# Block order of GpSimd's residual and bias additions in a fused graph attention and graph convolution kernel

## The chip, the cores and the metric

The kernel runs on one core of a Trainium2 chip. The metric is the device time of one execution in microseconds (us), the median of several runs. A core has five engines that run their own instruction streams side by side and wait for each other through semaphores: TensorE (PE: matmuls; PEld: its weight loads), VectorE (DVE), ScalarE (ACT), GpSimd (POOL) and SyncE (SP), which here only issues transfers (DMAs). They share an on-chip memory of 128 partitions (SBUF); matmuls write to a second one, PSUM, which GpSimd doesn't read here.

## What is computed

Two layers over 32 batches (B) of 512 nodes with 512 features (N = D = 512), in float32. Layer 0 is masked attention with 8 heads of 64, layer 1 a graph convolution with the symmetrically normalised adjacency. Each has a residual and a layer norm without weights.

```python
def _layernorm(x, axis=-1, eps=1e-5):
    m = jnp.mean(x, axis=axis, keepdims=True)
    v = jnp.var(x, axis=axis, keepdims=True)
    return (x - m) / jnp.sqrt(v + eps)

# layer 0
q, k, v = ((x @ W + b).reshape(B, N, 8, 64) for W, b in ((Wq, bq), (Wk, bk), (Wv, bv)))
scores = jnp.einsum('bihd,bjhd->bhij', q, k) / 8
scores = scores + jnp.where(adj == 0, -1e9, 0.0)[None, None]
out = jnp.einsum('bhij,bjhd->bihd', softmax(scores), v).reshape(B, N, 512)
x = _layernorm(x + out)
# layer 1
deg_inv_sqrt = jnp.where(deg > 0, rsqrt(deg), 0.0)      # deg = adj.sum(axis=1)
norm_adj = adj * deg_inv_sqrt[:, None] * deg_inv_sqrt[None, :]
x = _layernorm(x + jnp.einsum('nm,bmo->bno', norm_adj, x @ weight) + bias)
```

## The kernel before

The 512 nodes of a batch are four blocks of 128 (NT = 4, one block per 128 partitions); the eight heads are four pairs (G = 4), taken in the order 0, 2, 1, 3. Projections and the last product with the convolution's weight use a scheme of seven block products instead of eight (`seven`, `second`), whose pieces are written out and combined by VectorE, ScalarE and GpSimd.

The main loop (line 819) runs over all pairs of heads of all batches, 128 steps. Step k issues the scores of its own pair and the values (`values`, line 408) of the pair before it. In each of two halves of a step, eight score matmuls write two PSUM tiles `sc`; VectorE takes each into a tile `e` with the cap and the mask (line 384), ScalarE takes the exponential in place (line 387), and GpSimd adds the `e` tiles up in `acc` (`accumulate`, line 389), from which the softmax's sums are folded. There are two `sc` buffers in PSUM, so the second half's score matmuls wait until VectorE has emptied the first half's. Projections and other products use three PSUM buffers named `mm`.

Between the two score halves other work is placed. While the scores of batch b are made, the steps also hold the projections for batch b + 1 and the rest of batch b - 1. They are lists of pieces, `main` (seven pieces for the values, then seven and five or more for keys and queries), with side pieces put behind the piece of a given number by the dictionary `beside` (line 849). `cut` (line 769) deals the list over the four steps of a batch, eight matmul pieces to a step. Instructions are kept in the order of the program on each engine (`InOrder`, line 34; all of them appear under line 44 in the profile). The order of the program is thus the order of every engine's queue.

The side pieces that matter here come from `finish(b)` (line 498), which ends layer 0 of one batch:

- `inverse_all` makes the reciprocals of the softmax's sums, `inv`.
- `scale` (line 537, VectorE): the attention's output `yT`, block i, times `inv`. The profile shows it as `yT<-yT,inv`.
- `add` (line 544, GpSimd): plus the residual, `yT<-yT,xr`.
- `measure` (line 564, VectorE): mean and variance of each block, `st<-yT` and `mv<-st`.
- `root` (line 569): `ve` and `nmu` on VectorE, then reciprocal root `rstd` and `add` on GpSimd, all four blocks in one.
- `norm` (line 574, ScalarE): the normalised block `yT<-yT,add,rstd`, and its scaled, rounded high part `hi<-yT,dis`.
- `low` (line 592, VectorE): the low part that `hi` leaves, `lo<-yT,dis,hi`. TensorE multiplies the adjacency by both parts (`mm<-adjT,hi` and `mm<-adjT,lo`).
- `lift` (line 597, GpSimd): plus the layer 1 bias, `yT<-yT,b_r`.
- `grow` (line 600, ScalarE): times the root of the degree, `yT<-yT,rdeg`; layer 1 adds its products to this.

Each of these runs once per block, in the order that `block` (line 604) gives: 0, 1, 2, 3. They are placed like this:

```python
6: rest[6:] + f["scale"][:2], 7: f["scale"][2:] + f["add"],
8: measure[:2] + put_off, 9: measure[2:], 10: f["root"] + put_off, 11: norm[:1],
12: norm[1:2] + low[:1], 13: norm[2:3] + low[1:2], 14: norm[3:] + low[2:3],
15: low[3:] + f["lift"], 16: put_off + grow[:2], 17: put_off + grow[2:], 18: turn0 + f["judge"],
```

`put_off` is a held back accumulation of `e` tiles on GpSimd (`more`, line 784). Piece 7 is the first projection piece of keys and queries; it stands last in its step's share, so the next step's scores follow behind `add`. Piece 15 is again the last of its share, and the scores follow behind `lift`. In the projection pieces for keys and queries the piece with number 10 is the one in which VectorE makes `u` (line 358), and TensorE's piece 13 takes over the PSUM buffer that this frees.

The batches 0 to 29 pass through this dictionary. Batch 30 is finished in lists of its own (lines 864 to 880), and batch 31 in the lines from 919 on; it scales and adds in pairs of heads (`add_pair`) instead of with `scale` and `add`. `general` (line 952) stands by for inputs out of range and doesn't run here.

Of the kernel before, what the change touches and what calls it, by code (L numbers as in the profile page):

```python
# [49 lines left out]
def unshifted(  # L50
# [29 lines left out]
    B, N, D = x.shape  # L80
    NT = N // P
# [395 lines left out]
    def statistics(y, mv):  # L477
        st = small.tile([P, 6], F32, name="st")
        vector.bn_stats(st, y)
        vector.bn_aggr(mv, st)  # L480
# [17 lines left out]
    def finish(b):  # L498


        t = {}
# [60 lines left out]
                )  # L562

        def measure(i):
            if i == 0:
                t["mv"] = small.tile([P, NT, 2], F32, name="mv")
            statistics(YT[b][:, i, :], t["mv"][:, i, :])

# [35 lines left out]
        def block(f):  # L604
            return [(0, f, (i,)) for i in range(NT)]

        return dict(
            early=[(0.6, inverse, ((0,),))], late=[(0.6, inverse, ((1,),)), (0.6, turn_values, (ORDER[-1],))],
            pairs=[[(0, add_pair, (i, g)) for i in range(NT)] for g in ORDER],
            halves=[(0, root, (0, 2)), (0, root, (2, 2))],  # L610
            inverse=[(0.6, inverse_all, ())], scale=block(scale), add=block(add), measure=block(measure), root=[(0, root, ())],
            judge=[(0, judge, ())], norm=block(norm), low=block(low), lift=block(lift), grow=block(grow),
        )

    def weave(side, main):
# [203 lines left out]
    for k in range(S + 1):  # L819
        b, at = divmod(k, G)  # L820
        if at == 1:
# [10 lines left out]
            if b == 0:  # L832
# [10 lines left out]
                shares = cut(side, (4, 4, 4, 4))  # L843
            elif b < B - 1:
                f, c = finish(b - 1), convolve(b - 1)
                norm, low, grow, measure = f["norm"], f["low"], f["grow"], f["measure"]

# [11 lines left out]
                if b < B - 2:  # L859
                    side += put_off + s[:1] + put_off + s[1:3] + turn1[1:2] + s[3:4] + turn1[2:3] + s[4:5]  # L860
                    side += turn1[3:4] + s[5:6] + c["measure"][:1] + turn1[4:] + s[6:] + c["measure"][1:2]
                    rest = c["measure"][2:] + c["root"] + c["store"]
                    shares = cut(side, (8, 8, 8, 8))
                else:
                    held, h, last = c, s, finish(b)
                    scale, add = last["scale"], last["add"]
                    side += h[:1] + last["inverse"] + h[1:2] + scale[:2] + h[2:3] + scale[2:] + add
                    shares = cut(side, (8, 8, 8, 4))
            else:
                f, c, last = last, convolve(b - 1), finish(b)  # L870
                s, first, low, lift, pairs = c["second"], c["first"], f["low"], f["lift"], last["pairs"]
                within = low[:1]
# [47 lines left out]
    norm, low, lift, block, pairs, extend = end["norm"], end["low"], end["lift"], e["block"], end["pairs"], c["extend"]  # L920
# [310 lines left out]
```

## Time and profile before

| | us |
|---|---|
| median of 3 runs (lowest to highest) | 2856.01 (2855.47 to 2856.58) |
| the profiled execution | 2858.47 |
| its span, first to last instruction | 2856.4 |
| TensorE busy in the span | 2817.5 |
| VectorE busy | 2301.6 |
| GpSimd busy | 1846.0 |
| ScalarE busy | 1046.8 |

The mean granted clock of TensorE in the profiled execution was 0.997. The groups of instructions that the change concerns, all on tiles of 128 partitions by 512 float32 elements; smallest, median and largest duration are from the view of one tile's instructions, the busy time from the list of groups:

| instruction | engine | count | ns, min / median / max | busy us |
|---|---|---|---|---|
| `yT<-yT,inv` (scale) | VectorE | 124 | 676 / 1243 / 1759 | 159.3 |
| `yT<-yT,xr` (add) | GpSimd | 124 | 1263 / 1652 / 1730 | 192.8 |
| `st<-yT` (measure) | VectorE | 124 | 659 / 664 / 690 | 83.2 |
| `lo<-yT,dis,hi` (low) | VectorE | 124 | 732 / 1235 / 1621 | 150.0 |
| `yT<-yT,b_r` (lift) | GpSimd | 124 | 1269 / 1278 / 1745 | 171.2 |

Rows of the timeline give start, duration, engine, operation, output and inputs, the number of like instructions merged in the row, and in brackets how long the engine sat idle before and what ended that. Consecutive instructions of one engine overlap by some tens of ns in the records, so a step is read from one start to the next.

### The profile page before, as it was taken

Reading aid. Unit: us, or ns where it says so; the run is one execution under the profiler, and the core shown is the slowest. Engines: PE = TensorE matmul, PEld = TensorE weight load, DVE = VectorE, ACT = ScalarE, POOL = GpSimd, SP = SyncE. Lnnn points to the kernel's source line nnn. Section 1 sums busy time; section 2 is a strip of 40 time slices with the busy share of each in tenths; the row PEclk is TensorE's granted clock in tenths of the full one; section 3 lists DMA queues with packets and bytes.
Section 4 is the critical chain, followed back from the end, with each engine's and each line's share of the span. In section 5 each row is a group of like instructions: output and inputs, shape, how many; then the busy total and the mean of one; then the engine's idle time right before and its main releaser. Section 6 shows DMA issues by size and latency. Waiting matters only on the chain.

```text
span 2856.4 us, 34678 instructions
## 1 busy us (share of the span) xinstructions
PE 2817.5 (99%) x12540; PEld 1865.2 (65%) x12540; DVE 2301.6 (81%) x3201; ACT 1046.8 (37%) x1323; POOL 1846.0 (65%) x1174
## 2 busy tenths in 40 slices
PE   8999999999999999999999999999999999999997
PEld 6566666666666666666666666666666666666655
DVE  5878877888778887788887788877888778788787
ACT  2333333343333433333333334333343333333344
POOL 3666666766666666666666676666666666666666
PEclk9999999999999999999999999999999999999999
DMA  4111122111221112221112211122112222111211
GB/s 118 32 29 48 49 56 46 41 47 49 59 56 42 37 48 56 56 45 41 49 48 58 51 41 41 50 58 56 41 37 51 53 56 45 41 49 48 59 38 50
DMA packets 379108, 141.05 MB, mean 49 GB/s; under 512 B 277808, under 2 KB 345392, under 8 KB 378928
## 3 DMA queue, kind: packets, MB, share of 16 engines
q1 hardware_dynamic: 377776, 137.17, 20.1%
q8 instruction: 101, 1.65, 0.2%
q10 hardware_dynamic: 1152, 1.57, 0.2%
q14 instruction: 79, 0.65, 0.1%
HBM read 71.83 MB, written 33.55 MB: 37 GB/s over the span
## 4 chain that ended last, share of the span: by engine, by line
PE 78%; DVE 19%; issue 2%; POOL 0%; DMA 0%; ACT 0%; DVEq 0%; POOLq 0%; ACTq 0%
PE mm L44 52%; PE sc L44 13%; PE av L44 12%; DVE yT L44 5%; DVE e L44 5%; DVE st L44 3%; DVE acc L44 1%; DVE u L44 1%; DVE mv L44 1%; DVE yb L44 1%; DVE v L44 1%; DVE kq L44 1%; DVE xT L44 0%; DVE plainT L44 0%; POOL xT L44 0%
## 5 line engine op out<-in xcount | busy, mean ns | idle before, releaser
L44 ACT ACTIVATE e<-e 128x1024 f32<-128x1024 f32 x512 | 540.8, 1057 | 1166.2 <-DVE e L44 1137.2
L44 POOL TENSOR_TENSOR acc<-acc,e 128x1024 f32<-128x1024 f32 x248 | 588.9, 2375 | 188.3 <-ACT e L44 181.0
L44 DVE SCALAR_TENSOR_TENSOR e<-sc,maskT 128x1024 f32<-128x1024 f32 x512 | 597.5, 1207 | 22.1 <-PE sc L44 21.9
L44 PE MATMUL sc<-kq 64*128 64x512 f32 x2048 | 523.2, 623 | 3.5 <-DVE e L44 3.3
L44 PE MATMUL mm<-xT,wk 128*128 128x256 f32 x1792 | 476.3, 388 | 13.7 <-DVE u L44 11.3
L44 PE MATMUL av<-e,v 128*64 128x512 f32 x2048 | 467.9, 598 | 0.0
L44 PE MATMUL mm<-xT,wq 128*128 128x256 f32 x1792 | 460.7, 380 | 0.0
L44 POOL TENSOR_TENSOR acc<-e 128x1024 f32<-128x1024 f32 x126 | 297.2, 2358 | 230.4 <-ACT e L44 230.4
L44 PEld LDWEIGHTS mm<-xT,wk 128*128 128x128 f32 x1792 | 327.8, 190 | 143.1 <-issue 73.1
L44 PE MATMUL mm<-wv,xT 128*128 128x256 f32 x1792 | 404.3, 383 | 1.7 <-DVE xT L44 1.1
L44 PEld LDWEIGHTS mm<-wv,xT 128*128 128x128 f32 x1792 | 335.6, 190 | 72.3 <-issue 25.4
L44 PEld LDWEIGHTS mm<-xT,wq 128*128 128x128 f32 x1792 | 341.1, 190 | 46.5
L44 PEld LDWEIGHTS sc<-kq 64*128 64x128 f32 x2048 | 171.3, 186 | 290.7 <-issue 150.9
L44 PEld LDWEIGHTS av<-e,v 128*64 128x64 f32 x2048 | 135.5, 136 | 316.2 <-issue 293.4
L44 PE MATMUL mm<-w,zT 128*128 128x256 f32 x992 | 224.9, 379 | 0.7 <-ACT side L44 0.7
L44 POOL TENSOR_TENSOR rstd<-ve,minus_half 128x4 f32<-128x4 f32 (+1 forms) x66 | 66.2, 1003 | 232.5 <-DVE nmu L44 232.5
L44 DVE TENSOR_TENSOR kq<-u,mm 128x512 f32<-128x512 f32 x128 | 87.8, 686 | 156.5 <-PE mm L44 153.0
L44 POOL TENSOR_TENSOR yT<-yT,b_r 128x512 f32<-128x512 f32 x124 | 171.2, 1392 | 63.3 <-DVE lo L44 63.3
L44 PEld LDWEIGHTS mm<-w,zT 128*128 128x128 f32 x992 | 188.2, 190 | 28.1 <-issue 1.5
L44 POOL TENSOR_TENSOR yT<-yT,xr 128x512 f32<-128x512 f32 x124 | 192.8, 1584 | 18.8 <-DVE yT L44 18.8
L44 PE MATMUL mm<-adjT,hi 128*128 128x512 f32 x496 | 202.0, 407 | 0.0
L44 PE MATMUL mm<-adjT,lo 128*128 128x512 f32 x496 | 196.0, 395 | 0.9 <-DVE lo L44 0.9
(141 smaller groups left out, 3382.8 us busy)
## 6 DMA issues: line engine op xcount, KB each, us to landing
out_dram<-y SPq DMA_DIRECT2D x127, 256.0 KB, 2.1
x<-in_x_dram SPq DMA_DIRECT2D x248, 128.0 KB, 2.9
yT<-yb SPq DMA_DIRECT2D x496, 64.0 KB, 2.5
xr<-in_x_dram SPq DMA_DIRECT2D x122, 256.0 KB, 3.3
wk<-in_L_gnn_Wk_dram SPq DMA_DIRECT2D x8, 128.0 KB, 5.0
wq<-in_L_gnn_Wq_dram SPq DMA_DIRECT2D x8, 128.0 KB, 4.3
yT<-in_adj_dram SPq DMA_DIRECT2D x1, 1024.0 KB, 6.4
w<-in_L_gnn_weight_dram SPq DMA_DIRECT2D x2, 512.0 KB, 8.1
```

The source lines that it names most:

```text
L44: return self.tc.keep_in_program_order(op(*args, **kwargs))
```

## The change

`finish` gets a second way to list a function's blocks, `behind`, which takes the last block first: 3, 0, 1, 2. `add` uses it always, `measure`, `lift` and `grow` for all batches but the last. `scale`, `norm` and `low` keep the order 0, 1, 2, 3. `measure` makes its tile at the first call, whichever block that is for.

The slices of lists that the dictionary takes (`measure[:2]`, `grow[:2]`) are unchanged; they now hold the blocks 3 and 0, the others 1 and 2. GpSimd's first `add` reads what the last `scale` wrote, and its first `lift` overwrites what the last `low` read; with the queues in order the other three of each stand behind it.

```diff
         def measure(i):
-            if i == 0:
+            if "mv" not in t:
                 t["mv"] = small.tile([P, NT, 2], F32, name="mv")
             statistics(YT[b][:, i, :], t["mv"][:, i, :])
...
         def block(f):
             return [(0, f, (i,)) for i in range(NT)]
 
+        def behind(f):
+
+
+            return [(0, f, (i,)) for i in (NT - 1, *range(NT - 1))]
+
         return dict(
...
-            inverse=[(0.6, inverse_all, ())], scale=block(scale), add=block(add), measure=block(measure), root=[(0, root, ())],
-            judge=[(0, judge, ())], norm=block(norm), low=block(low), lift=block(lift), grow=block(grow),
+            inverse=[(0.6, inverse_all, ())], scale=block(scale), add=behind(add),
+            measure=block(measure) if b == B - 1 else behind(measure), root=[(0, root, ())],
+            judge=[(0, judge, ())], norm=block(norm), low=block(low),
+            lift=block(lift) if b == B - 1 else behind(lift), grow=block(grow) if b == B - 1 else behind(grow),
         )
```

## The prediction

> **What bounds the kernel now.** I read the page first: engine shares, then the chain that ended last.
>
> ```profile
> PE 2817.5 (99%) x12540; PEld 1865.2 (65%) x12540; DVE 2301.6 (81%) x3201; ACT 1046.8 (37%) x1323; POOL 1846.0 (65%) x1174
> PE 78%; DVE 19%; issue 2%; POOL 0%; DMA 0%; ACT 0%; DVEq 0%; POOLq 0%; ACTq 0%
> ```
>
> TensorE (PE) is busy nearly always, yet a fifth of the chain lies on VectorE (DVE). So there are places where TensorE just keeps up with, or waits for, VectorE. The chain over 1556 to 1592 us shows where:
>
> ```profile
> 1557.88 5.11 DVE yT L44 x4
> 1562.99 2.27 DVE e L44 x2
> ...
> 1574.92 0.77 DVE u L44 x2
> 1575.73 5.45 PE mm L44 x24
> ```
>
> From the four scalings (yT) on, VectorE works without a break for 17.8 us, until TensorE waits for its `u`. The stage repeats every 87.80 us (the first scaling starts at 1470.00, then 1557.80), 30 times, for the batches 0 to 29; batch 30 has it in the tail.
>
> The timeline around the scalings, each asked for in a narrow window, VectorE and GpSimd (POOL):
>
> ```profile
> 1556.13 2.36 POOL L44 TENSOR_TENSOR acc<-acc,e 128x1024 f32<-128x1024 f32 x1
> 1557.80 1.24 DVE L44 TENSOR_TENSOR yT<-yT,inv 128x512 f32<-128x512 f32 x1
> ...
> 1558.96 0.68 DVE L44 TENSOR_TENSOR yT<-yT,inv 128x512 f32<-128x512 f32 x1
> 1559.12 1.65 POOL L44 TENSOR_TENSOR yT<-yT,xr 128x512 f32<-128x512 f32 x1 [0.63 <-DVE yT L44]
> ...
> 1559.57 1.75 DVE L44 TENSOR_TENSOR yT<-yT,inv 128x512 f32<-128x512 f32 x1
> 1560.73 1.72 POOL L44 TENSOR_TENSOR yT<-yT,xr 128x512 f32<-128x512 f32 x1
> ```
>
> A scaling with no GpSimd instruction starting before it takes 0.68 us. The third and fourth, beside residual additions, take 1.75; the first, beside the end of an accumulation, 1.24.
>
> What this costs TensorE I read from the starts of its rows:
>
> ```profile
> 1558.81 1.99 PE L44 MATMUL sc<-kq 64*128 64x512 f32 x8
> 1560.73 3.65 PE L44 MATMUL av<-e,v 128*64 128x512 f32 x16
> 1564.32 2.13 PE L44 MATMUL sc<-kq 64*128 64x512 f32 x8
> 1566.37 1.13 PE L44 MATMUL mm<-xT,wk 128*128 128x256 f32 x4
> ...
> 1573.38 1.11 PE L44 MATMUL mm<-xT,wk 128*128 128x256 f32 x4
> 1574.33 1.03 PE L44 MATMUL mm<-xT,wq 128*128 128x256 f32 x4
> 1575.73 1.13 PE L44 MATMUL mm<-xT,wk 128*128 128x256 f32 x4 [0.38 <-DVE u L44]
> ...
> 1577.57 1.03 PE L44 MATMUL mm<-xT,wk 128*128 128x256 f32 x4
> ...
> 1583.03 3.65 PE L44 MATMUL av<-e,v 128*64 128x512 f32 x16
> 1586.69 2.26 PE L44 MATMUL sc<-kq 64*128 64x512 f32 x8
> 1588.88 1.13 PE L44 MATMUL mm<-xT,wk 128*128 128x256 f32 x4
> ```
>
> Eight undisturbed score matmuls take 1.92 us to the next start (1558.81 to 1560.73), the values 3.59 (to 1564.32). A projection piece (four `wk` and four `wq` matmuls) takes 1.73: 1568.20 to 1569.93 in the same view. Against that TensorE loses:
> - 0.13: second scores, 1564.32 to 1566.37 is 2.05
> - 0.62: the piece at 1573.38, 2.35 to the next; it waits for the PSUM buffer that `u` frees
> - 0.11: the next piece, 1.84
> - 0.07: values at 1583.03, 3.66 to the next
> - 0.27: scores at 1586.69, 2.19 to the next
>
> Sum 1.20 us per batch. Times 30: 36.0 us of 2856.4. This is what a faster VectorE can give back.
>
> **What the Trainium skill says.** "SBUF — State Buffer", "Who interferes with whom": a VectorE instruction with two SBUF inputs contends with a GpSimd instruction that reads SBUF, and one with at most one SBUF input outside the two-port modes does not. The trace agrees: scaling (`yT` and `inv`) ranges from 676 to 1759 ns; `e` (PSUM and the mask) takes 1.21 us whether or not an addition runs. "Perfetto Trace Analysis", "Tensor Engine Instruction (MATMUL, LD_WEIGHTS)": the profiler's matmul end is an estimate. The trace agrees in that busy intervals overlap (1558.81 plus 1.99 is after 1560.73), so I use starts. "TensorE: Matmul & The Clock Gate", "Architectural detail: the array is 16× 32×32, not 1× 128×128": VectorE, ScalarE and GpSimd queues are strictly first in, first out. The in-order rows agree, and it is why block 3 in front holds all the other blocks.
>
> **The change, part by part.** No instruction is added or removed. The sequences on TensorE, VectorE, ScalarE and SyncE keep their kinds and shapes; only block numbers turn from 0,1,2,3 to 3,0,1,2. On GpSimd the first addition waits for the last scaling (or low part), and the next three have no wait for VectorE left. SyncE's DMAs are in the same order.
>
> *Additions.* The third and fourth scalings fall from 1.75 to 0.68: 2 x 1.07 = 2.14 us less on VectorE. The first keeps its 1.24, since the accumulation started before it. Scalings then end near 1560.86. GpSimd starts at 1560.94 and needs 4 x 1.24 (steps of the uncontended additions, 1.27 long and overlapping slightly), so to 1565.9; before, to 1565.4. The accumulation behind it started at 1566.49, held by ScalarE's exponential, which now comes 2.1 us sooner; so it starts at about 1565.9. The additions' new delay costs nothing: the first measurement, of block 3, is wanted at about 1568.9 and its addition ends at 1562.2. Without that slack of over 6 us each late microsecond would hold VectorE.
>
> *VectorE downstream.* The scores' `e` begin at 1560.8 instead of 1562.92, when their matmuls (1558.81 to 1560.73) are just done. Transpose, fold, `yb` follow; `yb` waits for the values, over at 1564.3, and is not late. The second `e` pair then runs 1566.0 to 1568.3 instead of to 1570.45, the measurements and `u` to 1573.5 instead of 1575.7. TensorE, without its losses, wants the buffer at 1574.98. Slack 1.4 us: the 0.13, 0.62 and 0.11 go.
>
> *Measure and root.* Same instructions, other block order; the reciprocal roots of all four blocks still start after the last. They come 2 us sooner.
>
> *Low parts and bias additions.* Two of the four low parts run beside a bias addition (mean over the batches 1361 and 1600 ns against 739 for the free one). Free: 0.62 + 0.86 = 1.48 us less. The first stays at 1.22 (an accumulation is beside it). Walking the chain: root 1573.7, first `hi` 1576.6, last `hi` 1581.9 (ScalarE's row of norms, `hi` and `e` copies is now what is late), last low 1582.7, then `e`: first score buffer free at 1583.8. TensorE wants it at 1585.77. Slack 2 us: the 0.07 and 0.27 go.
>
> *Bias additions' end.* Four after the last low part: 1582.8 to 1587.9, against 1586.9 before. Behind them stands the accumulation that waited for an exponential until 1588.93. It starts at 1587.9, sooner still; ScalarE's `grow` comes over 5 us later. Nothing shown waits.
>
> *Batch 30 in the tail.* The additions wait for a scaling beside `y<-yT,e`, about 0.4 us later; the last low part is 0.46 shorter, and TensorE waits 0.91 for it. GpSimd's later work slides by up to 2.3 us, into 1.77 us of idle time at 2801.6. I take 0, bounds -0.5 and +1.
>
> *Unknown.* TensorE's first `adjT` step is 0.42 us long in every batch, with 0.23 later. If that is a wait on VectorE rather than TensorE's own, another 0.19 x 30 = 5.7 us goes. I take 0; lower end 5.7. At the other side, each wait carries about 0.10 us of slower restart and small brushes beside it, which may be TensorE's own: bounded in the first rival.
>
> Sum: 1.20 x 30 = 36.0 less. Profiled span 2856.4 - 36.0 = 2820.4; its execution was 2858.47, 2.07 around the span, and the median of the runs 2856.01, 2.46 below it. Taken from the median: **2820**.
>
> **The rivals.** *Half goes.* Restarts (three of 0.10) and the brush of 0.08 before the long wait, with the rest small, stay since TensorE has them anyway. Then about 0.73 x 30 = 22 goes: 2834. For it: every restart after other changes of operand also shows 0.10. Against: undisturbed second scores lack it.
>
> *Nothing moves.* The freed 3.6 us of VectorE were hidden by TensorE at 99%: 2856. For it, the page's share; against, the start-to-start losses above, present in all 30 batches. That the change doesn't reach the order of issue is excluded by the GpSimd sequence.
>
> *Slower: the root comes late.* Block 3 in front makes GpSimd idle, then run four in a row; an accumulation that is thereby late would stand ahead of the root, and root, norm, `hi`, low, `e` would all wait. It decides when the second scores of the next step lose over 0.93 us more than now (what is gained elsewhere); each microsecond beyond costs 30. With the root 2 us later than now: (2 - 0.93) x 30 = 32, 2888. For it: that chain has no idle step once the root starts. Against: GpSimd idled 2.85 us before the root, for VectorE.
>
> **How the numbers follow.** Full gain 0.70 (2820; own range 2813 to 2827), half 0.18 (2834, 2826 to 2844), nothing 0.05, slower 0.07. The range for 8 in 10 is 2811 to 2838: full gain with the `adjT` step taken at nearly its end, and most of half. About 0.2%, 5.7 us, is what a measurement of this kernel can tell from no change. Faster by more 0.88, within 0.05, slower 0.07.
>
> **What would show it.** The period falls from 87.8 to 86.6; the third and fourth scaling read 0.68, low parts two and four 0.74; PE shows no wait on DVE `u`; second scores take 1.92 to the next start. Scalings short with the period at 87.8 would mean VectorE's lead ends in another wait, root or `hi`; scalings still at 1.75 would break the contention argument itself.

## The result and the profile after

| | before | changed |
|---|---|---|
| median of 4 runs, us | 2856.3 | 2821.38 |
| lowest to highest | 2855.47 to 2857.94 | 2821.04 to 2821.77 |
| profiled execution | 2858.47 | 2821.64 |
| its span | 2856.4 | 2819.7 |
| from one batch's first scaling to the next | 87.80 | 86.60 |

The ratio is 0.9877, 95% interval 0.9864 to 0.9889. The predicted time was 2820.

The two medians differ by 34.9 us; the prediction took off 36.0. From the page of the changed kernel, the engine shares and the chain that ended last:

```profile
PE 2792.0 (99%) x12540; PEld 1874.8 (66%) x12540; DVE 2177.5 (77%) x3201; ACT 1050.1 (37%) x1323; POOL 1786.4 (63%) x1174
PE 97%; DVE 2%; POOL 0%; issue 0%; DMA 0%; ACT 0%; POOLq 0%; DVEq 0%; ACTq 0%
```

TensorE's busy share is 99% as before, so it does not show the gain. The chain does: VectorE's share fell from 19% to 2%. Over 1530 to 1620 us, a little more than one batch, it lies on TensorE throughout; three of its 17 pieces:

```profile
1543.85 1.92 PE sc L44 x8
1545.77 14.01 PE mm L44 x64
1559.78 1.92 PE sc L44 x8
```

The timeline of the changed kernel for the stage that the prediction shows, VectorE and GpSimd (the first scaling starts at 1537.27, in the kernel before at 1557.80):

```profile
1537.27 3.03 DVE L44 TENSOR_TENSOR yT<-yT,inv 128x512 f32<-128x512 f32 x4
1540.22 2.34 DVE L44 SCALAR_TENSOR_TENSOR e<-sc,maskT 128x1024 f32<-128x1024 f32 x2
...
1552.21 0.84 DVE L44 SCALAR_TENSOR_TENSOR u<-e,step,mm 128x256 f32<-128x256 f32 x2
...
1561.24 0.75 DVE L44 SCALAR_TENSOR_TENSOR lo<-yT,dis,hi 128x512 fp32r<-128x512 f32 x1 [0.66 <-ACT hi L44]
1561.91 2.35 DVE L44 SCALAR_TENSOR_TENSOR e<-sc,maskT 128x1024 f32<-128x1024 f32 x2
...
1540.38 4.98 POOL L44 TENSOR_TENSOR yT<-yT,xr 128x512 f32<-128x512 f32 x4 [2.43 <-DVE yT L44]
...
1562.08 4.98 POOL L44 TENSOR_TENSOR yT<-yT,b_r 128x512 f32<-128x512 f32 x4 [5.25 <-DVE lo L44]
```

The same rows in the kernel before:

```profile
1557.80 5.19 DVE L44 TENSOR_TENSOR yT<-yT,inv 128x512 f32<-128x512 f32 x4
...
1574.84 0.84 DVE L44 SCALAR_TENSOR_TENSOR u<-e,step,mm 128x256 f32<-128x256 f32 x2
...
1585.42 2.34 DVE L44 SCALAR_TENSOR_TENSOR e<-sc,maskT 128x1024 f32<-128x1024 f32 x2
```

The four scalings take 3.03 us instead of 5.19, and GpSimd idles 2.43 us ahead of its additions. Counted from the first scaling, `u` comes at 14.94 us instead of 17.04, and the scores' `e` behind the low parts at 24.64 instead of 27.62. TensorE in the same stage:

```profile
1543.78 1.99 PE L44 MATMUL sc<-kq 64*128 64x512 f32 x8
1545.70 1.13 PE L44 MATMUL mm<-xT,wk 128*128 128x256 f32 x4
...
1552.71 1.03 PE L44 MATMUL mm<-xT,wk 128*128 128x256 f32 x4
...
1554.44 1.03 PE L44 MATMUL mm<-xT,wk 128*128 128x256 f32 x4
...
1556.17 1.03 PE L44 MATMUL mm<-xT,wk 128*128 128x256 f32 x4
...
1561.63 3.65 PE L44 MATMUL av<-e,v 128*64 128x512 f32 x16
1565.21 1.99 PE L44 MATMUL sc<-kq 64*128 64x512 f32 x8
1567.13 1.13 PE L44 MATMUL mm<-xT,wk 128*128 128x256 f32 x4
```

All five losses are gone: both scores take 1.92 us to the next start, the values 3.58, the pieces 1.73, and no bracket shows a wait for `u`. The same holds in the other batches. A batch has 388 steps from one matmul's start to the next; averaged over 29 batches, only eight of them differ by more than 12 ns between the two kernels. All eight lie at these five places, and together they are 1.20 us.

The view of the tile's instructions in the changed kernel (smallest, median, largest duration in ns, first and last start):

```profile
L44 DVE TENSOR_TENSOR yT<-yT,inv x124: 677/680/1764, 151.7 to 2724.2; 128x512 f32<-128x512 f32 x124
L44 POOL TENSOR_TENSOR yT<-yT,xr x124: 1261/1278/1292, 154.8 to 2729.7; 128x512 f32<-128x512 f32 x124
...
L44 DVE SCALAR_TENSOR_TENSOR lo<-yT,dis,hi x124: 734/752/1233, 170.5 to 2748.7; 128x512 fp32r<-128x512 f32 x124
L44 POOL TENSOR_TENSOR yT<-yT,b_r x124: 1262/1278/1294, 176.5 to 2753.2; 128x512 f32<-128x512 f32 x124
```

The 36.7 us of span are accounted for: 29 periods of 1.20 (34.8), 1.21 from the last of these to batch 30's first scaling, 1.36 in the start before the first scaling, and 0.64 given back in the tail. The first two are the change: 36.0. The start has the same instructions in the same order in both kernels (it took 153.03 us before and 151.67 after); in the kernels below it took anywhere from 150.96 to 153.38 us, so the 1.36 is within the scatter.

### The profile page after: what moved, and what is told of

The parts are those of the page before. It is cut to its first block, busy times and chain, and to the rows that moved or that the text cites. A ratio compares the mean times of both kernels' runs of the same rounds, so it can differ in the third digit from the quotient of the medians.

```text
span 2819.7 us, 34592 instructions
## 1 busy us (share of the span) xinstructions
PE 2792.0 (99%) x12540; PEld 1874.8 (66%) x12540; DVE 2177.5 (77%) x3201; ACT 1050.1 (37%) x1323; POOL 1786.4 (63%) x1174
## 3 DMA queue, kind: packets, MB, share of 16 engines
q8 instruction: 101, 1.65, 0.2%
## 4 chain that ended last, share of the span: by engine, by line
PE 97%; DVE 2%; POOL 0%; issue 0%; DMA 0%; ACT 0%; POOLq 0%; DVEq 0%; ACTq 0%
PE mm L44 64%; PE sc L44 17%; PE av L44 16%; DVE e L44 1%; DVE xT L44 0%; DVE plainT L44 0%; POOL xT L44 0%; POOL acc L44 0%; DVE st L44 0%; DVE y L44 0%; DMA xr<-in_x_dram 0%; DVE lo L44 0%; DVE kq L44 0%; DVE lost L44 0%; DVE ve L44 0%
## 5 line engine op out<-in xcount | busy, mean ns | idle before, releaser
L44 PE MATMUL sc<-kq 64*128 64x512 f32 x2048 | 510.1, 616 | 3.6 <-DVE e L44 3.5
L44 PE MATMUL mm<-xT,wk 128*128 128x256 f32 x1792 | 469.7, 384 | 2.4 <-issue 2.0
L44 POOL TENSOR_TENSOR yT<-yT,b_r 128x512 f32<-128x512 f32 x124 | 154.6, 1279 | 167.7 <-DVE lo L44 167.7
L44 POOL TENSOR_TENSOR yT<-yT,xr 128x512 f32<-128x512 f32 x124 | 154.4, 1278 | 73.6 <-DVE yT L44 73.6
```

What stands on the lines that cost most here:

```text
L44: return self.tc.keep_in_program_order(op(*args, **kwargs))
```

## The experiments

Each is compared in five rounds with runs of the kernel before on the same chip, which gave 2855.24 to 2856.15 us as medians. For the changed kernel the 2821.38 us from above are used. Close cases are read from the period, the mean time from one batch's first scaling to the next; the kernels given with 86.60 agree in it within 0.01 us.

### One half alone

**Additions and measurements only.**

```diff
-            lift=block(lift) if b == B - 1 else behind(lift), grow=block(grow) if b == B - 1 else behind(grow),
+            lift=block(lift), grow=block(grow),
```

> Additions and measurements with block 3 in front; bias additions and grow in the old order 0, 1, 2, 3, so two low parts run beside bias additions again (1.4 and 1.6 us). Theory (only waits at a PSUM buffer cost time, and VectorE has slack after the scalings): the scores behind the low parts come 0.9 us later than in the changed kernel, the first score buffer is still free 1.2 us before TensorE wants it, so the period stays 86.6 and the time is 2821 to 2823. Rival (each microsecond that VectorE saves is worth the same, 36 us for 2.14 + 1.48 us): 2821 + 15 = 2836.

Measured: 2821.36 us, ratio 0.9879 (0.9863 to 0.9894), period 86.60. VectorE's timeline of this kernel, where the first scaling starts at 1538.46:

```profile
1559.09 2.05 DVE L44 SCALAR_TENSOR_TENSOR lo<-yT,dis,hi 128x512 fp32r<-128x512 f32 x2
...
1562.44 1.61 DVE L44 SCALAR_TENSOR_TENSOR lo<-yT,dis,hi 128x512 fp32r<-128x512 f32 x1 [0.67 <-ACT hi L44]
1563.97 2.34 DVE L44 SCALAR_TENSOR_TENSOR e<-sc,maskT 128x1024 f32<-128x1024 f32 x2
```

The low parts are slow again (1.38 and 1.61 us), `e` comes at 25.51, 0.87 later than in the changed kernel, and the time is the same. So with the additions moved, moving the bias additions is worth nothing that can be measured. `e` still comes earlier than the 27.62 of the kernel before, and that is early enough.

**Bias additions and grow only.**

```diff
-            inverse=[(0.6, inverse_all, ())], scale=block(scale), add=behind(add),
-            measure=block(measure) if b == B - 1 else behind(measure), root=[(0, root, ())],
+            inverse=[(0.6, inverse_all, ())], scale=block(scale), add=block(add),
+            measure=block(measure), root=[(0, root, ())],
```

> Bias additions and grow with block 3 in front; additions and measurements in the old order, so the third and fourth scaling take 1.75 us again. Theory: the losses of 0.13, 0.62 and 0.11 us per batch at the second scores and at u stay, the 0.07 and 0.27 behind the low parts go: 0.34 x 30 = 10 us less than before, 2846. Period 87.46. Rival (each saved microsecond of VectorE is worth the same): 1.48 of 3.62, 15 us less, 2841.

Measured: 2846.6 us, ratio 0.9967 (0.9955 to 0.9979), period 87.47. TensorE's timeline of this kernel:

```profile
1567.96 1.11 PE L44 MATMUL mm<-xT,wk 128*128 128x256 f32 x4
1568.90 1.03 PE L44 MATMUL mm<-xT,wq 128*128 128x256 f32 x4
1570.31 1.13 PE L44 MATMUL mm<-xT,wk 128*128 128x256 f32 x4 [0.38 <-DVE u L44]
...
1581.19 1.99 PE L44 MATMUL sc<-kq 64*128 64x512 f32 x8
1583.11 1.13 PE L44 MATMUL mm<-xT,wk 128*128 128x256 f32 x4
```

The wait for `u` is as before; the scores behind the low parts take the undisturbed 1.92. The halves alone gain 35 and 10 us, both at once 35: the second gain is contained in the first, because moving the additions also brings the low parts forward by about 2 us.

### The wait or the block order

```diff
+        def touch():
+            last = small.tile([P, 32], F32, name="last", bufs=1)
+            gpsimd.tensor_copy(last, YT[b][:, NT - 1, :32])
+
+        def touch_low():
+            last = small.tile([P, 32], F32R, name="last2", bufs=1)
+            gpsimd.tensor_copy(last, LO[b][NT - 1][:, :32])
...
+            inverse=[(0.6, inverse_all, ())], scale=block(scale), add=[(0, touch, ())] + block(add),
+            measure=block(measure), root=[(0, root, ())],
...
+            lift=block(lift) if b == B - 1 else [(0, touch_low, ())] + block(lift), grow=block(grow),
```

> All blocks in the old order 0, 1, 2, 3; ahead of the additions GpSimd copies 32 columns of the last scaled block, and ahead of the bias additions 32 columns of the last low part, into a small tile nobody reads. So the wait is as in the changed kernel, the block order as before. Theory (what counts is that GpSimd waits for the last scaling and low part): 2821 to 2823, scalings 0.68, period 86.6. Rival (the order of the blocks itself, that is which measurement or grow comes first, is part of the gain): above 2826.

Measured: 2821.22 us, ratio 0.9877 (0.9862 to 0.9892), period 86.60. The timeline of this kernel:

```profile
1537.04 3.05 DVE L44 TENSOR_TENSOR yT<-yT,inv 128x512 f32<-128x512 f32 x4
...
1540.15 0.21 POOL L44 COPY last<-yT 128x32 f32<-128x32 f32 x1 [2.42 <-DVE yT L44]
...
1540.50 1.27 POOL L44 TENSOR_TENSOR yT<-yT,xr 128x512 f32<-128x512 f32 x1
```

A copy of 0.21 us that waits does all that the block order does. So the order in which the blocks are added and measured is no part of the gain; what counts is that GpSimd's queue stands until VectorE is through.

### How much VectorE may lose

**Half of the scalings' gain given back.**

```diff
-            inverse=[(0.6, inverse_all, ())], scale=block(scale), add=behind(add),
-            measure=block(measure) if b == B - 1 else behind(measure), root=[(0, root, ())],
+            inverse=[(0.6, inverse_all, ())], scale=block(scale), add=[(0, add, (i,)) for i in (1, 0, 2, 3)],
+            measure=block(measure) if b == B - 1 else [(0, measure, (i,)) for i in (1, 0, 2, 3)], root=[(0, root, ())],
```

> Additions and measurements in the order 1, 0, 2, 3, bias additions and grow with block 3 in front as in the changed kernel. GpSimd then starts after the second scaling; one scaling runs beside an addition and takes 1.75 instead of 0.68, so half of the 2.14 us comes back. Theory (slack of about 1.3 us at u, 2 us behind the low parts): all of it fits into the slack, 2821 to 2824, no wait of TensorE for u. Rival (the gain is in proportion to VectorE's saving): 1.07 of 3.62 us lost, 2821 + 11 = 2832.

Measured: 2822.27 us, ratio 0.9881 (0.9866 to 0.9896), period 86.60. The median scaling durations are 1227, 678, 677 and 1750 ns. One slow scaling per batch costs nothing in the period.

**Both given back in part.** The edit is the one just shown together with the first one, `lift=block(lift), grow=block(grow)`.

> Additions and measurements in the order 1, 0, 2, 3, bias additions and grow in the old order: one scaling at 1.75 and two low parts at 1.4 and 1.6 come back, 1.07 + 1.48 = 2.55 of the 3.62 us that the change saves on VectorE. Theory (slack of 1.4 us at u, of 2.06 us at the scores behind the low parts, where 1.07 + 0.87 = 1.94 us are used): still 2820 to 2824, period 86.6 to 86.7. Rival (in proportion): + 25, 2846.

Measured: 2824.03 us, ratio 0.9891 (0.9875 to 0.9908), period 86.70. The timeline of this kernel, VectorE and TensorE, first scaling at 1538.17:

```profile
1563.16 1.61 DVE L44 SCALAR_TENSOR_TENSOR lo<-yT,dis,hi 128x512 fp32r<-128x512 f32 x1 [0.71 <-ACT hi L44]
1564.69 2.34 DVE L44 SCALAR_TENSOR_TENSOR e<-sc,maskT 128x1024 f32<-128x1024 f32 x2
...
1566.12 2.10 PE L44 MATMUL sc<-kq 64*128 64x512 f32 x8
1568.15 1.13 PE L44 MATMUL mm<-xT,wk 128*128 128x256 f32 x4
```

This is the edge: the time is just above the expected range, the period at its upper end. `e` comes at 26.52, 1.88 later than in the changed kernel, and the scores take 2.03 to the next start instead of 1.92. 2.55 of the 3.62 us that the change saves on VectorE are lost again, and of the 1.20 us per batch only 0.10.

**VectorE loaded from outside.** Two kernels add statistics that nobody reads, two or four a batch (`i < 1` or `i < 3`):

```diff
             statistics(YT[b][:, i, :], t["mv"][:, i, :])
+            if b < B - 2 and (i == NT - 1 or i < 1):
+                vector.bn_stats(small.tile([P, 6], F32, name="st"), YT[b][:, i, :])
```

> The changed kernel with two more statistics per batch on VectorE (batches 0 to 29), of blocks 3 and 0, written to a tile nobody reads: 2 x 0.6 = 1.2 us more ahead of u. Theory (slack of about 1.3 us until TensorE wants the buffer that u frees): next to nothing, 2821 to 2825, TensorE's wait for u at most a brush. Rival (VectorE's time counts in proportion, 36 us for 3.62): + 12, 2833.

> The changed kernel with four more statistics per batch on VectorE (batches 0 to 29), one for each block: 2.4 us more ahead of u. Theory: 2.4 less the slack of 1.3 is 1.1 us late at u, with restart some 1.2 us per batch, 36 us: 2857, and TensorE waits for u again; the first two cost nothing, the second two nearly all. Rival (in proportion): + 24, 2845.

Measured: two, 2820.5 us, ratio 0.9875 (0.986 to 0.989), period 86.60. Four, 2856.53 us, ratio 1.0001 (0.9992 to 1.0009), period 87.74. TensorE's timeline of the kernel with four:

```profile
1572.24 1.03 PE L44 MATMUL mm<-xT,wk 128*128 128x256 f32 x4
1573.10 1.03 PE L44 MATMUL mm<-xT,wq 128*128 128x256 f32 x4
1575.00 1.13 PE L44 MATMUL mm<-xT,wk 128*128 128x256 f32 x4 [0.87 <-DVE u L44]
```

The first 1.2 us cost nothing (the time is even 0.5 us under the expected range), the next 1.2 us cost the whole gain. `u` starts 17.30 us after the first scaling there, 2.36 later than in the changed kernel, and the step up to the waiting piece (1573.10 to 1575.00) is 1.04 too long. The difference is the slack at `u`, the time by which VectorE may be late before TensorE has to wait: 1.3 us.

### What slows a scaling

**GpSimd reads beside the scalings.** Two additions of zero to the bias row, ahead of the residual additions:

```diff
+        def beside_scale():
+            if b < B - 2:
+                for _ in range(2):
+                    gpsimd.tensor_add(b1_r, b1_r, sel[:, 0, 1:2].to_broadcast([P, D]))
...
-            inverse=[(0.6, inverse_all, ())], scale=block(scale), add=behind(add),
+            inverse=[(0.6, inverse_all, ())], scale=block(scale), add=[(0, beside_scale, ())] + behind(add),
```

> The changed kernel with two more GpSimd additions of 128 x 512 ahead of the residual additions, batches 0 to 29; they add zero to the bias row and wait for nothing on VectorE, so they run beside the scalings. Theory (a GpSimd instruction that reads this memory beside a scaling is the cause): scalings take 1.7 us again in part, VectorE loses 2.0 to 2.5 us, u is late by 0.7 to 1.2 us, the time is 2845 to 2858. Rival (what counts is where the residual additions stand): 2821 to 2824.

Measured: 2833.6 us, ratio 0.9921 (0.9908 to 0.9935), period 86.99 to 87.0. Outside the expected 2845 to 2858, and clearly above the rival's 2824. The timeline of this kernel:

```profile
1544.16 4.72 DVE L44 TENSOR_TENSOR yT<-yT,inv 128x512 f32<-128x512 f32 x4
...
1544.80 2.93 POOL L44 TENSOR_TENSOR b_r<-b_r,sel 128x512 f32<-128x512 f32 x2
...
1560.47 1.03 PE L44 MATMUL mm<-xT,wq 128*128 128x256 f32 x4
1561.62 1.13 PE L44 MATMUL mm<-xT,wk 128*128 128x256 f32 x4
1562.59 1.03 PE L44 MATMUL mm<-xT,wq 128*128 128x256 f32 x4
```

The mechanism was right, the size too large: the second and third scaling take 1.52 us, not 1.7, so VectorE loses 4.72 - 3.03 = 1.69 us, not 2.0 to 2.5. `u` starts 16.57 us after the first scaling, 1.63 later than in the changed kernel. Less the slack of 1.3, 0.3 is left: the step up to the waiting piece is 0.29 too long and the step behind it 0.10. That is 0.40 in the period, 12 us in 30 batches.

**GpSimd only writes.** The same with ten memsets into a tile `spare` of 128 x 128:

```diff
+                spare = small.tile([P, P], F32, name="spare", bufs=1)
+                for _ in range(10):
+                    gpsimd.memset(spare, 0.0)
```

> The changed kernel with ten memsets of 128 x 128 on GpSimd ahead of the residual additions, batches 0 to 29, some 2 us that only write and run beside the scalings. Theory with the rule that a VectorE instruction with two inputs from this memory meets only GpSimd instructions that read it: scalings stay at 0.68, 2821 to 2824. Rival (any GpSimd instruction beside a scaling slows it): as with reads, above 2840.

Measured: 2820.94 us, ratio 0.9879 (0.9863 to 0.9894), period 86.60. The timeline:

```profile
1536.62 3.03 DVE L44 TENSOR_TENSOR yT<-yT,inv 128x512 f32<-128x512 f32 x4
...
1537.24 2.56 POOL L44 MEMSET spare<- 128x128 f32 x10
```

The memsets run for 2.56 us beside the scalings and slow none of them, nor are they slowed: each of the 300 takes 0.20 or 0.21 us. Together with the kernel that reads, this agrees with the Trainium skill ("SBUF — State Buffer", "Who interferes with whom"), which lets a two-input instruction of VectorE contend with GpSimd instructions that read this memory and not with those that only write it.

### The tail

Batch 30 takes the old order again: in `add`, `measure`, `lift` and `grow`, `block` is used for `b >= B - 2`.

> The changed kernel with the old block order for batch 30, whose end lies in the tail; batches 0 to 29 as changed. From the start of batch 30's first scaling to the end of the span the kernel before took 97.26 us, the changed one 97.90. Theory (the four bias additions in a row push the last accumulations in the tail past TensorE's sums): back to 97.0 to 97.3, period 86.6, time some 0.6 us under the changed kernel, 2820 to 2821. Rival (the 0.64 comes from elsewhere, such as the additions' delay, or from nothing): tail stays at 97.9.

Measured: 2820.66 us, ratio 0.9877 (0.9861 to 0.9894), tail 97.47 us. That lies between the two expectations, and it is inconclusive: the four kernels with statistics, additions or memsets leave batch 30 exactly as the changed kernel has it, and their tails are 97.34, 97.25, 97.26 and 97.23. The 0.64 us of one trace is as large as the scatter between equal tails. No version tried has a shorter period than the changed kernel. The one with two statistics a batch has a median 0.9 us lower, but its trace is shorter only in the start (150.96 against 151.67 us) and in the tail (97.34 against 97.90), where its work is the same.

## Why the prediction was right

- *Where the time is lost.* The five losses read from start to start, 1.20 us per batch, are what went: the period fell by 1.20. The prediction was right because it priced TensorE's losses and not VectorE's saving. The latter, 2.14 + 1.48 = 3.62 us per batch, would have given 109 us in 30 batches. (The pages show 124.1 us less of VectorE's busy time. The prediction overlooked one small instruction, `low<-inv`, whose mean fell from 1.01 to 0.19 us; no step of TensorE changed by it, so the forecast lost nothing.)
- *The last microsecond.* That the median came within 1.4 us of 2820 is partly luck: the start alone took between 150.96 and 153.38 us in these kernels.
- *Scalings.* The third and fourth take 0.68, as forecast; the first kept 1.23, since the accumulation ahead of the additions still runs beside it. Low parts two and four went to 0.74 and 0.75.
- *GpSimd's later work.* The additions ended 8.1 us after the first scaling as computed; the accumulation behind them started with no idle time, earlier than before. GpSimd idled 2.91 us before the root, for VectorE, so the rival in which GpSimd makes the root late had nothing to stand on.
- *Slack.* 1.4 us at `u` was predicted, 1.3 measured by loading VectorE. At the scores behind the low parts 2 us were predicted; 1.88 was just too much.
- *The half rival.* It took the restarts of 0.10 us and the brushes (steps lengthened by less than 0.1 us) for TensorE's own. They vanished with the waits, so they belong to the waits. The 0.42 us step at the first `adjT` matmul stayed at 0.42 in every kernel, whether VectorE was early or late: nothing shows it to be a wait on VectorE, and the lower end that it was given was not needed.
- *Two parts.* The prediction let the low parts' relief carry 0.34 us per batch. The runs say this share comes from whichever part brings VectorE forward first. The working of the sum did not show it, and the first experiment does.
- *Tail.* Taken at 0 with -0.5 and +1; 0.64 in the one trace, inside the scatter.

## What to carry to other kernels

When one engine is nearly always busy, look for the places where it starts late, step by step from start to start, and count those. That sum bounds what ending these waits can give, however much time the helper saves: here 1.20 us per batch out of 3.62. Before adding a wait on a helper's queue, measure what stands behind it: here GpSimd could idle 2.4 us, because nothing waited for its additions at their new end, 8.1 us after the first scaling instead of 7.6. And a gain of two edits that relieve the same chain is not the sum of their gains: try each alone.

## What the runs showed of the hardware

- *A wait of TensorE can cost a fixed 0.10 us beyond its length.* Delays of 0.54 us (kernel before, at `u`), 0.29 (with reads) and 1.04 (four statistics) are each followed by one matmul step that is 0.10 too long. So is the delay of 0.17 between score matmuls in the kernel before. At the edge it is the same even for a brush: there one step grew from 422 to 433 ns and the next long one from 422 to 526. It is not so everywhere: in the kernel before, 0.08 us at the piece ahead of the wait for `u` and 0.07 at the values have no such step behind them.
- *A slowed scaling is not a scaling at a lower rate.* In the kernel before, an addition ran from 1559.12 for 1.65 us, to 1560.77, and the scaling beside it, started at 1559.57, ended at 1561.32, 0.55 us after the addition. In the kernel with reads an addition ended at 1546.29, the scaling at 1546.84, again 0.55 after it. It is so throughout: in the kernel before, all 182 scalings and low parts that took over 0.9 us ended 0.54 to 0.55 us after the GpSimd instruction beside them, whether they took 1.2 us or 1.75. Where the scaling started first, it kept its 0.68 us, and the addition took 1.65 and ended 1.12 to 1.14 us after it. So the one that starts second seems to stand until the other is over and then to run at its full rate.
